# Layer 3's per-batch mixing on half-height, half-width products, with one bias product per block

## The chip, the cores and the metric

One core of a Trainium2 chip. The metric is the time of one execution in microseconds (us) on the device. All data are float32. The core has TensorE (PE, whose weight loads are listed apart as PEld), VectorE (DVE), ScalarE (ACT), GpSimd (POOL) and SyncE (SP), which here only issues DMAs.

## The reference, cut to what matters

Four layers follow each other on an activation x of 32 batches, 64 channels and 1024 features. Each adds to x a function of x and of a conditioning vector of 128 numbers per batch. Layers 0 and 3 first mix the channels of each batch with a matrix of its own:

```python
att = jax.nn.softmax((h @ W2 + b2) / T, axis=-1)        # 32 batches x 8
agg_w = jnp.einsum('bk,koi->boi', att, weight[..., 0])  # a 64x64 matrix per batch
agg_b = att @ bias_k                                    # 64 biases per batch
out = jnp.einsum('boi,bih->boh', agg_w, x) + agg_b[:, :, None]
```

In layer 3, whose mixing is changed, what comes out goes into a feed-forward part: an up product from 1024 to 2048 and 512 features, a down product back to 1024, a gate that sums the two largest of 8 logits, and a layer norm. Layers 1 and 2 mix by a grouped convolution. Layer 2's feed-forward part sends each row (a channel of a batch) to two of 16 experts, and gathers the two results per row at the end.

## The kernel before, in words

The 2048 rows (32 batches x 64 channels) lie in 16 tiles of 128 rows, so that a tile holds two batches: batch 2j in partitions 0 to 63 and batch 2j+1 in partitions 64 to 127. The work of a tile is named by j, its 8 chunks of 128 features by c.

Layer 3 goes in 4 blocks b of 4 tiles (t = 0 to 3). `blended` (L541) makes the mixed activation of a block, transposed: for a tile it multiplies a bias product (L547: `ones` of 8 rows by `bbs[t]`, which `mixed_bias` (L214) has made on GpSimd out of the attention weights and `bk3`), copies that to SBUF on ScalarE (L549), and then takes, for each chunk, the 128x128 piece of x as the stationary operand and `aw[:, t, :]` as the streamed one (L554). `aw` for a tile is 128x128 with the two batches' 64x64 matrices on its diagonal and zeros elsewhere, which `mixing` (L195) has laid out during layer 2 and stored in DRAM (`awd`). Four chunks go to one bank of PSUM; VectorE adds the bias and writes the sum into one of four quarters of y (L555). `quarters` (L515, its adds at L517 to L520) then makes four sums and differences of quarters, which the seven-product scheme of `seven` (L899) needs in the up (L954, products at L964) and down products (L1000, products at L1019).

Block 0 is mixed at the end of layer 2's part. There `gather` (L528) loads a tile of x3 and fetches the two expert results per row by indirect DMAs on GpSimd's queue (`fetch`, L525; L526), `merge` (L535) adds the three on VectorE (L537) and stores the sum as x4 (L538); its tiles come from `slot_b`, the pool `pb` of 8 buffers (L76), which also holds `aw0` (L817) and the layer-2 features yT of the last tiles until `base2` (L665, products at L670, adds at L676, store of x3 at L678) has used them. At most two gathers are asked for ahead (L820, L828). Once block 0 is mixed the pools of the early layers are closed, and layer 3's tiles lie where they were: gw (L840), aw (L854) and the up weights (`prepared`, L933) are loaded on SyncE's queue behind the stores of layer 2.

Blocks 1 to 3 are mixed by `mixed` (L851) in the middle of the block before: `down(b, 1, ...)` calls `meanwhile` after its second product "2" (L1027), and that calls `mixed(b + 1)` and `gate(b + 1)` (L858, products at L864). `mixed` loads the x4 tiles with `loaded` into a tag `xm` of two buffers, so that the load of the third tile waits until the first has been multiplied. The gate's copy `gs` (L867) has one buffer; `best` (L871) reads it at the start of the next block.

The order in which each engine's instructions stand in its queue isn't written out by hand: the framework sets it when the program is built, by the order of the source and by what it estimates to be ready, and it assigns buffers of a pool as it goes. An engine then works through its queue in that order and waits on semaphores.

The other names that the prediction uses: L611 is layer 2's routing product (80 streamed columns), L744 a transpose, L754 the expert products (64 rows at a time, the two halves of the array by turns), L915 to L921 the sums of `seven` (u_u, v_u, v_d), L842 and L844 loads of gamma and beta.

Of the kernel before, what the change touches and what calls it, by code (L numbers as in the profile page):

```python
# [28 lines left out]
F32 = mybir.dt.float32  # L29
# [4 lines left out]
ALU = mybir.AluOpType  # L34
AX = mybir.AxisListType

P = 128
D = 1024
NT = 16
NC = D // P  # L40
HF = 512
TB = 512
# [4 lines left out]
KC = 8  # L47
# [11 lines left out]
QUARTER = {(0, 0): 0, (1, 0): 1, (1, 1): 2, (0, 1): 3}  # L59
# [5 lines left out]
def four_layers(ctx: ExitStack, tc: tile.TileContext, a: dict, out: bass.AP):  # L65
    nc = tc.nc

    cst = ctx.enter_context(tc.tile_pool(name="cst", bufs=1))
    small = ctx.enter_context(tc.tile_pool(name="small", bufs=2))
# [9 lines left out]
    def slot_a(name):  # L79
        return pa.tile([P, D], F32, tag="a", name=name)  # L80

    def slot_b(name):
        return pb.tile([P, D], F32, tag="b", name=name)

    def bank(name, shape=(P, HF), dtype=F32):
        return psp.tile(list(shape), dtype, tag="ps", name=name)

    def const(name, src, shape, eng=None):
        t = cst.tile(list(shape), F32, name=name)
        (eng or nc.gpsimd).dma_start(out=t, in_=src)  # L90
        return t
# [6 lines left out]
    ones = cst.tile([P, P], F32, name="ones")  # L98
# [25 lines left out]
    att = {}  # L124
    with tc.tile_pool(name="mlp", bufs=1) as mp:
        mlp = {}
        for n in (0, 3):
            mlp[n] = {}
            for k, shape in (("W0", (P, P)), ("b0", (P, 1)), ("W1", (P, P)), ("b1", (P, 1)), ("W2", (P, KC))):
                t = mp.tile(list(shape), F32, name=f"{k}_{n}")  # L130
                nc.sync.dma_start(out=t, in_=a[f"{k}_{n}"])
                mlp[n][k] = t
            t = mp.tile([NB, KC], F32, name=f"b2_{n}")
# [4 lines left out]
        for n in (0, 3):  # L138
            m = mlp[n]
            ps = bank(f"mlp0_{n}", (P, NB))  # L140
# [3 lines left out]
            ps = bank(f"mlp1_{n}", (P, NB))  # L144
# [3 lines left out]
        for n in (0, 3):  # L148
            ps = bank(f"mlp2_{n}", (NB, KC))
# [15 lines left out]
            ps = bank(f"attT_{n}", (P, NB))  # L165
# [48 lines left out]
    def mixed_bias(n, j, bk, eng):  # L214

        bb = small.tile([KC, 2, 64], F32, tag="row", bufs=8, name=f"bb_{n}_{j}")
        eng.tensor_tensor(
            bb,
            att[n][:KC, ts(j, 2), None].to_broadcast([KC, 2, 64]),
            bk[:, None, :].to_broadcast([KC, 2, 64]),  # L220
            ALU.mult,
        )
        return bb.rearrange("k b o -> k (b o)")
# [28 lines left out]
    with tc.tile_pool(name="q", bufs=1) as qp, tc.tile_pool(name="w", bufs=NC) as wq:  # L252
# [6 lines left out]
        with tc.tile_pool(name="l0", bufs=1) as lp, tc.tile_pool(name="s0", bufs=2) as sp:  # L259
# [7 lines left out]
            zs, lhs, whs, whTs, rows, bbs, cbs = {}, {}, {}, {}, {}, {}, {}  # L267
# [102 lines left out]
            aw = lp.tile([P, NT, P], F32, name="aw_0")  # L370
# [9 lines left out]
            ps = bank("rsum", (KC, E0 + P))  # L380
# [132 lines left out]
    bk3 = const("bk_3", a["bk_3"], (KC, 64))  # L513

    def quarters(t, r):  # L515
        tt = nc.vector.tensor_tensor
        tt(t[0], r[3], r[0], ALU.subtract)  # L517
        tt(t[1], r[2], t[0], ALU.subtract)
        tt(t[2], r[2], r[3], ALU.subtract)
        tt(t[3], r[1], t[1], ALU.subtract)  # L520
# [7 lines left out]
    def gather(j, tile3):  # L528
        got = [tile3(f"m{i}_{j}") for i in range(3)]
        nc.sync.dma_start(out=got[0], in_=x3[j])  # L530
        for k in range(2):
            fetch(got[1 + k], outs[:, :], slot[:, k, j : j + 1])
        return got

    def merge(j, got):  # L535
# [2 lines left out]
        nc.sync.dma_start(out=x4[j], in_=got[0])  # L538
        return got[0]

    def blended(b, aw, tiles, bbs):  # L541

        y = [slot_a(f"y3_{b}_{q}").rearrange("p (c t) -> p c t", t=HT) for q in range(8)]
        for t in range(4):
            j = 4 * b + t
            ps = bank(f"ab_{j}", (P, P))
            nc.tensor.matmul(ps, ones[:KC, :], bbs[t], start=True, stop=True)  # L547
            ab = small.tile([P, P], F32, tag="row", bufs=8, name=f"abs_{j}")
            nc.scalar.copy(ab, ps)  # L549
            xt = tiles(t)  # L550
            for h in range(2):
                ps = bank(f"mix_{j}_{h}", (P, 4, P))
                for c in range(4):
                    nc.tensor.matmul(ps[:, c, :], xt[:, ts(4 * h + c, P)], aw[:, t, :], start=True, stop=True)  # L554
                nc.vector.tensor_tensor(  # L555
                    y[QUARTER[h, t // 2]][:, :, ts(t % 2, P)], ps, ab[:, None, :].to_broadcast([P, 4, P]), ALU.add
                )
        quarters(y[4:8], y[0:4])
        return y

# [3 lines left out]
    with (  # L564
# [212 lines left out]
        for j in range(NT + 1):  # L777
# [13 lines left out]
            if j == 4:  # L791
                aw = [wp.tile([P, NT // 2, P], F32, tag="bg", bufs=3, name=f"aw3_{i}") for i in range(2)]
# [23 lines left out]
                base2(*late.pop(0))  # L816
        aw0 = slot_b("aw3_now")[:, : 4 * P].rearrange("p (t o) -> p t o", o=P)  # L817
        nc.sync.dma_start(out=aw0, in_=awd[:, 0:4, :])
        bbs = [mixed_bias(3, j, bk3, nc.gpsimd) for j in range(4)]
        got = [gather(j, slot_b) for j in range(2)]  # L820
        for j in range(AMID - 2, AMID):
            for n in range(2):
# [2 lines left out]
        def now(j):  # L825
# [3 lines left out]
            return t  # L829

        y = blended(0, aw0, now, bbs)

    early.close()
    l3 = ctx.enter_context(ExitStack())
    lp = l3.enter_context(tc.tile_pool(name="l3", bufs=1, reuse_waits="tile"))
# [10 lines left out]
    def loaded(j, name, bufs):  # L846
        t = wp.tile([P, D], F32, tag=name, bufs=bufs, name=f"{name}_{j}")
        nc.sync.dma_start(out=t, in_=x4[j])
        return t

    def mixed(b):  # L851

        aw = lp.tile([P, 4, P], F32, tag="aw", name=f"aw_{b}")
        nc.sync.dma_start(out=aw, in_=awd[:, ts(b, 4), :])  # L854
        bbs = [mixed_bias(3, j, bk3, nc.gpsimd) for j in range(4 * b, 4 * b + 4)]
        return blended(b, aw, lambda t: loaded(4 * b + t, "xm", 2), bbs)

    def gate(b, y):  # L858

        gp = bank(f"gp_{b}", (P, 2, HT))  # L860
        for half in range(2):
            for c in range(NC):
                q = ds(32 * (c % 4), 32)
                nc.tensor.matmul(  # L864
                    gp[q, half, :], gw[:, c, :], y[QUARTER[c // 4, half]][:, c % 4, :], start=(c < 4), stop=(c >= 4)
                )
        gs = lp.tile([P, TB], F32, tag="gs", name=f"gs_{b}")  # L867
        nc.scalar.copy(gs, gp.rearrange("p h t -> p (h t)"))
        return gs
# [216 lines left out]
    gs = gate(0, y)  # L1086
    for b in range(NBL):
        tot = [wp.tile([P, D], F32, tag="tot", bufs=4, name=f"tot_{b}_{t}") for t in range(4)]
        hs = [up(b, 0, y, None)]
        dgs = best(b, gs)  # L1090
        hs.append(up(b, 1, y, None))
        sg = spread_best(b, dgs)
        hs += [up(b, g, y, None) for g in range(2, HG)]
        down(b, 0, hs, tot, lambda: None)
        hs = []
        got = None
        for g in range(HG, NG):
            if b + 1 < NBL:
                j = 4 * b + 4 + g - HG
                if got:  # L1100
                    merge(j - 1, got)
                got = gather(j, merged) if g < HG + 4 else None
            hs.append(up(b, g, y, sg))
        ahead = []

        def meanwhile():
            if b + 1 < NBL:
                ahead.append(mixed(b + 1))
                ahead.append(gate(b + 1, ahead[0]))

        xs = residual(b)
        down(b, 1, hs, tot, meanwhile)
        if ahead:
            y, gs = ahead
        finish(b, tot, xs)
# [87 lines left out]
```

## Time and profile before

| | us |
|---|---|
| median of 3 runs | 1860.04 (1858.42 to 1861.30) |
| the profiled execution | 1869.54 |
| its span (first to last instruction) | 1867.8 |
| TensorE busy in it | 1740.9 (93%) |
| VectorE busy | 807.9 (43%) |
| mixing products of layer 3, blocks 1 to 3 (L554, 192 instructions) | 24.4 |
| the same, block 0 (64 instructions) | 11.1 |
| bias products (L547, 32 instructions) | 8.0 |
| bias adds (L555, 32 instructions) | 21.6 |

Times in the views are microseconds from the start of the span, unless ns is said. A row of a timeline gives start, length, engine, line of the kernel, operation, the tile written and those read, the size, and how many instructions the row merges; in square brackets stands how long the engine was idle before it and what ended that. A row of the chain gives start, length and what the time went to; "issue" is time for which the profile shows no cause. TensorE's lengths are from entry to the modelled end, so that a row's length holds a tail that overlaps the next row: what an instruction costs is read from start to start. A float32 product is two instructions on TensorE, each with a weight load.

### The profile page before, as it was taken

How to read it: one execution, taken by the hardware profiler on the slowest of the kernel's cores; microseconds unless marked ns; L12 is line 12 of the kernel's file. 1: busy time of each engine (PE TensorE's matmuls, PEld its weight loads, DVE VectorE, ACT ScalarE, POOL GpSimd, SP SyncE). 2: the span in 40 equal slices, each digit the busy share in tenths (PEclk: the TensorE clock that was granted, in tenths of full speed). 3: DMA queues.
4: the chain of work that ended last, by engine and by line, in shares of the span. 5: the costliest groups of instructions: out<-in, count | busy, mean ns of one | idle time of the engine just before them, and what ended most of it. 6: DMA issues, size and time to landing. Idle time of an engine off the chain costs nothing.

```text
span 1867.8 us, 20908 instructions
## 1 busy us (share of the span) xinstructions
PE 1740.9 (93%) x7526; PEld 1166.0 (62%) x7526; DVE 807.9 (43%) x1700; ACT 203.0 (11%) x547; POOL 600.6 (32%) x628
## 2 busy tenths in 40 slices
PE   7997779989999999898879999999999999999996
PEld 6576657766776433585357567486585685684862
DVE  1577799836655333463243361022541123620223
ACT  1100044200000122010000100000010000000000
POOL 2245535542432553244223142023141132320230
PEclk9999889989999999999989999999999999999998
DMA  8894321056662599888876574445564444644432
GB/s 297 265 280 85 58 68 46 1 147 192 188 177 87 184 355 353 292 297 299 280 254 215 160 241 148 150 150 162 176 209 158 148 154 140 232 152 152 147 96 96
DMA packets 185910, 340.48 MB, mean 182 GB/s; under 512 B 20432, under 2 KB 91872, under 8 KB 185808
## 3 DMA queue, kind: packets, MB, share of 16 engines
q1 hardware_dynamic: 171712, 295.76, 50.3%
q0 software_dynamic: 14096, 43.39, 7.1%
q8 instruction: 60, 0.98, 0.2%
q14 instruction: 42, 0.34, 0.1%
HBM read 238.28 MB, written 83.89 MB: 172 GB/s over the span
## 4 chain that ended last, share of the span: by engine, by line
PE 71%; DMA 11%; issue 7%; DVE 5%; POOL 3%; SPq 2%; ACT 0%; POOLq 0%; DVEq 0%; ACTq 0%
PE p_d L1019 23%; PE p_u L964 22%; PE o L670 8%; PE conv L239 5%; DMA m<-x 4%; PE oo L480 3%; PE lr L611 2%; PE fold L358 1%; DMA x<-m 1%; PE ex L754 1%; DMA g<-x 1%; DMA m<-outs,slot 1%; POOL x L489 1%; POOL lo L473 1%; PE mix L554 1%
## 5 line engine op out<-in xcount | busy, mean ns | idle before, releaser
L1019 PE MATMUL p_d<-dn,h 128*128 128x512 f32 x1120 | 487.4, 596 | 7.2 <-DVE v_d L921 3.8
L1019 PEld LDWEIGHTS p_d<-dn,h 128*128 128x128 f32 x1120 | 213.1, 191 | 274.3 <-issue 267.8
L964 PE MATMUL p_u<-y,up 128*128 128x256 f32 x1680 | 366.7, 380 | 6.0 <-DVE v_u L921 6.0
L964 PEld LDWEIGHTS p_u<-y,up 128*128 128x128 f32 x1680 | 319.3, 191 | 53.0 <-DVE v_u L921 7.2
L670 PE MATMUL o<-base,yT 128*128 128x512 f32 x512 | 225.5, 595 | 0.6 <-DVE eo L757 0.4
L670 PEld LDWEIGHTS o<-base,yT 128*128 128x128 f32 x512 | 95.4, 191 | 118.5 <-issue 115.0
L239 PE MATMUL conv<-cw,g 128*128 128x128 f32 x1024 | 129.3, 288 | 4.7 <-DMA g<-x 3.2
L239 PEld LDWEIGHTS conv<-cw,g 128*128 128x128 f32 x1024 | 126.7, 205 | 5.3 <-DMA g<-x 3.4
L480 PE MATMUL oo<-cbt,lo 128*128 128x512 f32 x256 | 103.6, 405 | 4.1 <-POOL lo L473 3.9
L480 PE MATMUL oo<-cbt,hi 128*128 128x512 f32 x256 | 104.5, 408 | 0.0
L977 POOL TENSOR_TENSOR raw<-u_u,v_u 128x256 f32<-128x256 f32 x40 | 31.5, 788 | 211.1 <-DVE v_u L921 211.0
L964 PE MATMUL p_u<-y,r 128*128 128x256 f32 x240 | 62.9, 414 | 24.3 <-DVE v_u L921 22.2
L537 DVE TENSOR_TENSOR m<-m,m 128x1024 f32<-128x1024 f32 x32 | 39.3, 1228 | 101.9 <-DMA m<-x 84.2
L676 DVE TENSOR_TENSOR xo<-x,o 128x256 f32<-128x256 f32 x64 | 35.4, 594 | 105.1 <-PE o L670 93.0
L526 POOL DMA_INDIRECT m<-outs,slot x32 | 38.4, 1200 | 125.8 <-DVE m L537 90.1
L921 DVE TENSOR_TENSOR v_u<-e_u,p_u 128x256 f32<-128x256 f32 x40 | 16.8, 419 | 136.2 <-PE p_u L964 136.2
L992 POOL TENSOR_TENSOR h<-h 128x256 f32<-128x256 f32 x40 | 29.5, 738 | 137.4 <-DVE h L986 100.8
L964 PE MATMUL p_u<-y,s 128*128 128x256 f32 x320 | 72.2, 379 | 0.0
L964 PEld LDWEIGHTS p_u<-y,r 128*128 128x128 f32 x240 | 49.3, 209 | 35.6 <-DVE v_u L921 24.6
L330 POOL TENSOR_TENSOR x<-x,bias 128x512 f32<-128x512 f32 x32 | 37.1, 1177 | 102.7 <-DMA g<-x 99.6
L921 DVE TENSOR_TENSOR v_d<-e_d,p_d 128x512 f32<-128x512 f32 x16 | 10.9, 687 | 127.4 <-PE p_d L1019 127.4
L964 PEld LDWEIGHTS p_u<-y,s 128*128 128x128 f32 x320 | 60.8, 190 | 8.3
(243 smaller groups left out, 2092.7 us busy)
## 6 DMA issues: line engine op xcount, KB each, us to landing
dn<-ds SPq DMA_DIRECT2D x160, 256.0 KB
up<-us SPq DMA_DIRECT2D x60, 512.0 KB
outs<-eo SPq DMA_DIRECT2D x48, 512.0 KB
dn<-in_dn_dram SPq DMA_DIRECT2D x96, 256.0 KB
g<-x SPq DMA_DIRECT2D x256, 64.5 KB
up<-in_up_dram SPq DMA_DIRECT2D x30, 512.0 KB
ds<-sum SPq DMA_DIRECT2D x20, 512.0 KB
us<-s SPq DMA_DIRECT2D x20, 512.0 KB
```

The costliest lines, as they stand in the source:

```text
L239: nc.tensor.matmul(ps[:, g, :], rows[:, 4 * b + g, ds(w, P)], cwt[:, g, w, :], start=(w == 0), stop=(w == 1))
L330: nc.gpsimd.tensor_tensor(xh(j, h), xh(j, h), halved(bias1[:, ts(h, HF)]), ALU.add)
L480: nc.tensor.matmul(po, terms[j][i][:, c, :], cbt[c][:, ts(n, HF)], start=(c == 0 and i == 0), stop=(c == NC - 1 and i == 1),)
L526: nc.gpsimd.indirect_dma_start(out=dst, out_offset=None, in_=src, in_offset=rows_of(at))
L537: nc.vector.tensor_tensor(got[0], got[0], got[1 + k], ALU.add)
L611: nc.tensor.matmul(ps, yT[j][:, c, :], ra2[:, c, :], start=(c == 0), stop=(c == NC - 1))
L670: nc.tensor.matmul(po, yT[j][:, c, :], base[c][:, ts(n, HF)], start=(c == 0), stop=(c == NC - 1))
L676: nc.vector.tensor_tensor(new, old[:, ts(n, 64), :], add, ALU.add)
L964: nc.tensor.matmul(ps[0], ws[i][:, k, c, :], y[RHS[p]][:, c, :], start=(start and c == 0), stop=(c == 3), skip_group_check=not start,)
L977: nc.gpsimd.tensor_tensor(raw[:, 1, 1], m["u"], m["v"], ALU.add)
L992: tt(h[:, 4], h[:, 1], h[:, 3], ALU.add)
L1019: nc.tensor.matmul(ps[q], hs[k][:, HLHS[p], ts(q, P)], ws[k], start=(start and k == 0), stop=(k == HG - 1), skip_group_check=not start,)
```

## The change

In `blended`, the bias of a block is one product: `block_bias` makes all 8 batches' weighted biases in one GpSimd operation, in a tile of 8 rows and 512 columns, one TensorE product of 512 columns follows, and four ScalarE copies. Each chunk of a tile is multiplied as two products of 64 rows and 64 streamed columns: partitions 0 to 63 by the first batch's matrix, partitions 64 to 127 by the second's, into two banks of PSUM, one per batch, each with all 8 chunks. The zeros of `aw` are no longer multiplied. VectorE's add takes one batch and four chunks at a time, so there are four of 128x256 per tile where there were two of 128x512. The new bias tile is a buffer of `slot_b` in block 0, and of the tag `gs` in the others.

```diff
+    def block_bias(b, t):
+        bb = t[:KC, : 4 * P].rearrange("k (t o) -> k t o", o=P)
+        nc.gpsimd.tensor_tensor(
+            bb.rearrange("k t (h o) -> k (t h) o", h=2),
+            att[3][:KC, ts(b, 8), None].to_broadcast([KC, 8, 64]),
+            bk3[:, None, :].to_broadcast([KC, 8, 64]),
+            ALU.mult,
+        )
+        return bb
+
     def blended(b, aw, tiles, bbs):
 
         y = [slot_a(f"y3_{b}_{q}").rearrange("p (c t) -> p c t", t=HT) for q in range(8)]
+        pa_ = bank(f"ab_{b}", (P, 4, P))
+        nc.tensor.matmul(pa_, ones[:KC, :], bbs.rearrange("k t o -> k (t o)"), start=True, stop=True)
+        abq = [small.tile([P, P], F32, tag="row", bufs=8, name=f"abs_{b}_{t}") for t in range(4)]
+        for t in range(4):
+            nc.scalar.copy(abq[t], pa_[:, t, :])
         for t in range(4):
             j = 4 * b + t
-            ps = bank(f"ab_{j}", (P, P))
-            nc.tensor.matmul(ps, ones[:KC, :], bbs[t], start=True, stop=True)
-            ab = small.tile([P, P], F32, tag="row", bufs=8, name=f"abs_{j}")
-            nc.scalar.copy(ab, ps)
+            ab = abq[t]
             xt = tiles(t)
+            ps = [bank(f"mix_{j}_{g}", (P, NC, 64)) for g in range(2)]
+            for c in range(NC):
+                for g in range(2):
+                    q = ds(64 * g, 64)
+                    nc.tensor.matmul(ps[g][:, c, :], xt[q, ts(c, P)], aw[q, t, q], start=True, stop=True)
             for h in range(2):
-                ps = bank(f"mix_{j}_{h}", (P, 4, P))
-                for c in range(4):
-                    nc.tensor.matmul(ps[:, c, :], xt[:, ts(4 * h + c, P)], aw[:, t, :], start=True, stop=True)
-                nc.vector.tensor_tensor(
-                    y[QUARTER[h, t // 2]][:, :, ts(t % 2, P)], ps, ab[:, None, :].to_broadcast([P, 4, P]), ALU.add
-                )
+                for g in range(2):
+                    q = ds(64 * g, 64)
+                    nc.vector.tensor_tensor(
+                        y[QUARTER[h, t // 2]][:, :, ds(t % 2 * P + 64 * g, 64)],
+                        ps[g][:, ts(h, 4), :],
+                        ab[:, None, q].to_broadcast([P, 4, 64]),
+                        ALU.add,
+                    )
         quarters(y[4:8], y[0:4])
         return y
...
-        bbs = [mixed_bias(3, j, bk3, nc.gpsimd) for j in range(4)]
+        bbs = block_bias(0, slot_b("bb3_0"))
...
-        bbs = [mixed_bias(3, j, bk3, nc.gpsimd) for j in range(4 * b, 4 * b + 4)]
-        return blended(b, aw, lambda t: loaded(4 * b + t, "xm", 2), bbs)
+        return blended(b, aw, lambda t: loaded(4 * b + t, "xm", 2), block_bias(b, lp.tile([P, TB], F32, tag="gs", name=f"bb3_{b}")))
```

## The prediction

> **What bounds the kernel now.** I read the page's totals and its chain first, then the timeline of TensorE around the mixing of blocks 1 to 3, then rows that show what a half-array product costs, then the handover from layer 2 to layer 3, where block 0 is mixed.
>
> ```profile
> PE 1740.9 (93%) x7526; PEld 1166.0 (62%) x7526; DVE 807.9 (43%) x1700; ACT 203.0 (11%) x547; POOL 600.6 (32%) x628
> ...
> PE 71%; DMA 11%; issue 7%; DVE 5%; POOL 3%; SPq 2%; ACT 0%; POOLq 0%; DVEq 0%; ACTq 0%
> ```
>
> TensorE is busy for 93% and is 71% of the chain, so what it is spared inside layer 3 is worth its full time, unless another wait comes up there. Now the timeline of TensorE in block 1 (start, length, ..., number of instructions):
>
> ```profile
> 1044.90 0.48 PE L547 MATMUL ab<-bb,ones 8*128 8x128 f32 x2
> 1045.31 2.05 PE L554 MATMUL mix<-aw,xm 128*128 128x128 f32 x16
> 1047.29 0.48 PE L547 MATMUL ab<-bb,ones 8*128 8x128 f32 x2
> 1047.71 2.05 PE L554 MATMUL mix<-aw,xm 128*128 128x128 f32 x16
> 1049.69 0.48 PE L547 MATMUL ab<-bb,ones 8*128 8x128 f32 x2
> 1050.75 2.02 PE L554 MATMUL mix<-aw,xm 128*128 128x128 f32 x16 [0.57 <-DMA xm<-x]
> 1052.70 0.48 PE L547 MATMUL ab<-bb,ones 8*128 8x128 f32 x2
> 1053.15 2.02 PE L554 MATMUL mix<-aw,xm 128*128 128x128 f32 x16
> 1055.11 1.50 PE L864 MATMUL gp<-y,gw 128*32 128x256 f32 x24
> ```
>
> Each product shows as two instructions (8 chunks, x16), each with a weight load of its own. A tile's bias product takes 0.41 us until the next row starts, a tile's mixing 1.98. From the first bias product to the gate (L864) it is 10.21 us; blocks 2 and 3 have 10.33 and 10.46. The third tile waits 0.57 us for xm: there are two buffers, its load is issued at 1047.39 when the first tile is done with one, and lands in time for 1050.75, 3.36 us later. That wait is what counts below.
>
> **Part 1: the mixing on TensorE.** 16 instructions of 128 rows and 128 streamed columns per tile become 32 of 64 rows and 64 columns. Two things must be known: what paces such instructions, and whether the two halves run side by side.
>
> ```profile
> 504.25 1.91 PE L611 MATMUL lr<-ra,yT 128*128 128x80 f32 x16
> 505.99 0.33 PE L642 MATMUL rk<-both,before 128*128 128x16 f32 x2
> ...
> 632.21 1.99 PE L754 MATMUL ex<-bg,bTs 64*128 64x512 f32 x8 [0.29 <-ACT bTs L746]
> 634.13 0.33 PE L744 MATMUL bT<-ident,bin 128*128 128x128 f32 x1
> ```
>
> L611 streams only 80 columns, and its 16 still take 1.74 us, 0.109 each, against 0.112 for the mixing with 128 (the loads of a tile take 1.86 us for 16, one 0.19: 1.67/15 = 0.111). So the pace is that of the weight load of 128 columns, and fewer streamed columns gain nothing. L754 multiplies 64 rows at a time on alternate halves, as the change will: 8 instructions of 512 columns end within 1.92 us, 0.24 each, where full-height ones of 512 columns take 0.43 (L670: 64 from 746.27 to 773.94). So halves run side by side, and their four first loads take 0.30 us together where one takes 0.18: two at a time. I take 32 instructions in pairs at 0.112 a pair, 1.79 us a tile, what the 16 take today: **no gain from the halves**. The lower bound is that the streams alone pace it (64/128 of 0.107 a pair, 0.86 a tile), against which L611 speaks; the upper that loads do not pair when the stream is short, 32 x 0.112 = 3.57 a tile.
>
> [...]
>
> **Part 2: one bias product per block.** Four of 0.41 go (1.64 us); one of 512 columns comes: 0.41 + 2 x (0.43 - 0.11) = 1.05 us. The tiles then follow each other without a change between, which spares about 0.1 us of entry and 0.1 of exit at each; these are in the 1.98.
>
> **Sum for blocks 1 to 3**, from the first bias instruction: bias to 1.05; tile 0 to 2.94 (0.1 entry + 1.79); its buffer's load is issued at 3.04 and lands for 6.40; tile 1 to 4.73; tile 2 6.40 to 8.29, with 1.67 us of waiting; tile 3's load, issued at 4.83, is there at 8.19; tile 3 to 10.08; gate at 10.18 against 10.21. The product saved is **eaten by the xm load**, for the first tile now frees its buffer 0.55 us later, behind the longer bias product. Blocks 2 and 3, whose fourth tile also waits for its load, gain some 0.1 each. All three: -0.2 us. Lower bound, if the streams pace it: tile 0 ends at 2.0, the load lands at 5.5, tiles 2 and 3 run to 7.5: -2.7 a block, -8 in all.
>
> VectorE: 8 adds of 128x512 (0.598 from start to start when queued) become 16 of 128x256 (L921, one of that size out of PSUM, lasts 0.419; less the 0.094 by which L555's 0.692 exceeds its pitch: 0.325), +0.4 us a block. It has idle time beside the mixing (9.64 of 13.3 us busy). Both halves of a tile now share banks, and the adds may have to wait for the whole tile: then the last four end at about 10.1 + 4 x 0.325 = 11.4, ahead of the last gate products, which today start at 12.70 after two instructions of the down product. Nothing. Were that cover gone, up to 1.3 us a block. GpSimd (four of 0.39 to one of four times the length) and ScalarE (four copies of 0.266 in a row while tile 0 is mixed) are idle there. The bias's new tile shares the one buffer of gs, long read by then, and is read before the next gate copy.
>
> **Part 3: block 0.** There the bias takes one of the 8 buffers of pool b (line 76). Two views, GpSimd's and then the chain:
>
> ```profile
> 758.23 0.95 POOL L526 DMA_INDIRECT m<-outs,slot  x1 [0.30 <-issue]
> 761.46 0.94 POOL L526 DMA_INDIRECT m<-outs,slot  x1 [2.29 <-DVE m L537]
> 765.07 0.94 POOL L526 DMA_INDIRECT m<-outs,slot  x1 [2.66 <-DVE m L537]
> ```
>
> ```profile
> 784.85 0.32 SPq L678
> ...
> 787.86 6.80 DMA r<-in_up_dram
> 794.66 0.14 issue
> 794.80 1.98 PE p_u L964 x8
> ```
>
> Held at that time: yT of tiles 12 and 13 (base2, until 774) and aw0. That leaves five: two m0 and three fetches. The trace agrees: fetches 1 to 3 go back to back (755.67, 756.98, 758.23), the fourth waits for the first merge add (759.97 + 1.23). With one buffer less, the third does: 761.46 instead of 758.23. It landed after 4.17 us (762.40), so now at 765.63; its add goes from 763.57 to 765.65, and the fifth fetch, which waited for that add, slips by 2.1 with it. By way of its adds and the seventh fetch (773.12) hang the add at 780.47, base2's adds queued behind it on VectorE, the store of x3 (784.85, L678), and behind it on SyncE gw, aw and the first up weights, for which TensorE waits 1.70 us until 794.80. After that it is busy (33.5 of 34 us). I take **+2.1**. Bounds: +4.1, if the sixth fetch must wait for the fourth's add as well; -1.7, if base2's adds come to stand ahead of the stalled merge add, so that the weights land early and the gate's end (793.1) decides. The shorter bias (0.7 us before tile 3) and the 12 queued adds (+0.4) lie beside the weights' 6.80 us.
>
> Forecast: -0.2 + 2.1 = +1.9 on the profiled execution, 1869.54 us (span 1867.8). That one lies 9.5 above the median of the runs, 1860.04, so I carry the difference over: 1862.
>
> **Rivals.**
> (B) *Loads do not pair*: 3.57 us a tile; gate at 1.05 + 0.1 + 14.3 + 0.1 = 15.5, so +5.3, +5.2, +5.0, and 2 to 3 in block 0 (two tiles fit ahead of 782.8): +18, **1878**, slower. The point from which it decides is 2.0 us a tile. For it: no row shows 64-row loads with so short a stream. Against: L754's loads in pairs. It is also the case that the halves do not do what the change says.
> (C, D) *VectorE's queue in block 0's up products shifts.* From 820 to 990 the merge adds of later blocks wait for their loads (84.2 us, 12 times) with v_u queued behind them, and TensorE waits for v_u 22.2 us, 6 times, longest 10.8. Their places are set when the program is built, from costs that this change alters. One wait more is 3.7 us by the mean: **1866**, slower (C); one or two fewer, or the bound of Part 1: 1862 - 7.4, **1854**, faster (D).
>
> **Chances.** Forecast 0.50 (own range 1857 to 1867; of it 0.37 within 0.2%, 0.11 above, 0.02 below), B 0.16, C 0.14, D 0.20 (0.17 faster, 0.03 same). Faster than 1856.3: 0.19; within 0.2%, about what a measurement can tell: 0.40; slower than 1863.8: 0.41. The range 1854 to 1879 reaches from D's middle to B and leaves out some 0.15.
>
> **What would show it.** Mixing rows at some 1.8 us a tile (3.6: B; under 1.2: D); a third tile that waits 1.2 us or more for xm; gate within 0.3 us of 10.2 after the first bias row; the third fetch of block 0 waiting for a merge add and the first p_u some 2 us later against the end of the expert stage; TensorE's waits for v_u near 22 us. If those move by over 4 us, the forecast is wrong for a reason that the change's own operations do not hold.

## The result, and the profile after

The change makes the kernel slower: a median of 1885.79 us over 5 runs (1880.82 to 1889.59) against 1860.04 (1858.42 to 1864.11), a ratio of 1.0133 with a 95% interval of 1.0113 to 1.0154. The forecast was 1862, and the time lies above the range that was given (1854 to 1879). The profiled execution of after took 1889.59 us (span 1887.8), 20 more than that of before, and the stages below are compared between these two. By the medians the change costs 25.7 us: the profile of before lay 9.5 above its median, that of after 3.8, so the account below is of 20 of them.

The page's totals after, for those of before:

```profile
PE 1749.4 (93%) x7758; PEld 1171.5 (62%) x7758; DVE 811.3 (43%) x1732; ACT 201.6 (11%) x547; POOL 602.8 (32%) x616
...
PE 45%; DMA 8%; DVE 4%; issue 1%; SPq 0%; ACT 0%; DVEq 0%; POOLq 0%
```

TensorE is as busy as before, which hides the loss: its instructions have become longer in some stretches. The shares of the chain add up to only 58% here, so I go by stages instead. From the start of the last expert product to the first up product of block 0 it was 49.0 us and is 58.5: +9.5. The stretch from the first bias product of a block's mixing to the last gate product was 13.0, 13.1 and 13.2 us in blocks 1 to 3 and is 17.3, 18.0 and 16.5: +12.6. What lies ahead of that last expert product moved by +1.7, all the rest by -3.8, and the sum is 20.

TensorE's timeline in block 1 after, for the one shown of before:

```profile
1055.01 1.12 PE L555 MATMUL ab<-bb,ones 8*128 8x512 f32 x2
1056.06 3.79 PE L567 MATMUL mix<-aw,xm 64*128 64x64 f32 x64
1061.39 7.09 PE L567 MATMUL mix<-aw,xm 64*128 64x64 f32 x64 [1.54 <-DVE y L571]
1068.41 2.68 PE L882 MATMUL gp<-y,gw 128*32 128x256 f32 x24
1071.03 1.12 PE L1037 MATMUL p_d<-dn,h 128*128 128x512 f32 x2
```

The first 64 instructions, two tiles, take 3.79 us, a tail included: 1.8 us a tile, as forecast. Then TensorE waits, as forecast too: the third tile starts 6.38 us after the bias product (forecast 6.40). The bracket puts the end of that wait to VectorE's adds, the releaser that was last by the profile. But in all three blocks of after the third tile starts 0.135 us after the last semaphore update of its load (1061.255 in block 1), and so it does in before, so it is the load that ends the wait. What the forecast had no term for comes then: the same 64 instructions take 7.09 us, and the gate's 24 take 2.68 where they took 1.50. They run at half the clock: the record of the granted clock has 0.50 from 1060.62 to 1070.86. In block 2 the clock falls ahead of the wait, at 1320.0, within the first two tiles:

```profile
1317.38 4.70 PE L567 MATMUL mix<-aw,xm 64*128 64x64 f32 x64
1322.67 7.09 PE L567 MATMUL mix<-aw,xm 64*128 64x64 f32 x64 [0.59 <-DVE y L571]
```

A table of the three blocks' stretches shows the clock (start and end, length, busy time of TensorE, its loads, VectorE, ScalarE, GpSimd, then the granted clock, the DMA share and GB/s):

```profile
1055.00:1072.70 17.70, 16.16 (x166) 12.37 (x165) 10.32 (x22) 0.77 (x4) 0.00 (x0) 0.71 0.49 163
1316.30:1334.90 18.60, 18.01 (x166) 13.64 (x166) 11.26 (x23) 0.88 (x5) 0.00 (x0) 0.63 0.48 158
1578.30:1595.40 17.10, 15.05 (x166) 11.35 (x166) 10.35 (x22) 0.87 (x5) 2.36 (x1) 0.80 0.37 126
```

The column to read is the one after GpSimd's: 0.71, 0.63 and 0.80, in blocks where before has 1.00 throughout:

```profile
1044.90:1058.20 13.30, 12.72 (x108) 9.78 (x107) 9.64 (x14) 1.06 (x4) 0.00 (x0) 1.00 0.60 184
```

GpSimd's timeline in block 0 after:

```profile
757.37 0.95 POOL L526 DMA_INDIRECT m<-outs,slot  x1 [22.27 <-issue]
758.62 0.95 POOL L526 DMA_INDIRECT m<-outs,slot  x1 [0.30 <-issue]
763.27 0.95 POOL L526 DMA_INDIRECT m<-outs,slot  x1 [3.70 <-DVE m L537]
765.76 0.94 POOL L526 DMA_INDIRECT m<-outs,slot  x1 [1.55 <-DVE m L537]
768.96 0.94 POOL L526 DMA_INDIRECT m<-outs,slot  x1 [2.25 <-DVE m L537]
775.11 0.94 POOL L526 DMA_INDIRECT m<-outs,slot  x1 [5.21 <-DVE m L537]
782.51 0.94 POOL L526 DMA_INDIRECT m<-outs,slot  x1 [6.45 <-DVE m L537]
788.80 0.94 POOL L526 DMA_INDIRECT m<-outs,slot  x1 [5.35 <-DVE m L537]
```

Every fetch from the third on waits for a merge add, and the last three go one at a time: fetch, landing, add, next fetch. The eighth goes at 788.80 where it went at 775.32. Until its add is done TensorE stands idle for 9.5 us. Later the load of gw lands at 802.28, and the gate's 32 products then run at half the clock (0.50 from 784.14 to 808.03): 3.64 us where they took 1.97, so that up to 1.7 of the 9.5 us that block 0 loses are the clock's.

### The profile page after: what moved, and what is told of

Same layout as the page of the kernel before. It is cut to its first block, busy times and chain, and to the rows that moved or that the text cites. A ratio compares the mean times of both kernels' runs of the same rounds, so it can differ in the third digit from the quotient of the medians.

```text
span 1887.8 us, 21396 instructions
## 1 busy us (share of the span) xinstructions
PE 1749.4 (93%) x7758; PEld 1171.5 (62%) x7758; DVE 811.3 (43%) x1732; ACT 201.6 (11%) x547; POOL 602.8 (32%) x616
## 4 chain that ended last, share of the span: by engine, by line
PE 45%; DMA 8%; DVE 4%; issue 1%; SPq 0%; ACT 0%; DVEq 0%; POOLq 0%
PE p_d L1037 22%; PE p_u L982 20%; DMA m<-x 4%; DMA x<-m 2%; PE mix L567 2%; DVE m L537 1%; DMA m<-outs,slot 1%; DVE tot L1095 1%; PE gp L882 1%; DMA r<-in_up_dram 1%; DVE st L1089 0%; DMA dn<-gd 0%; DMA gw<-in_gw_dram 0%; DVE tot L1072 0%; DMA xm<-x 0%
## 5 line engine op out<-in xcount | busy, mean ns | idle before, releaser
L480 PE MATMUL oo<-cbt,lo 128*128 128x512 f32 x256 | 104.3, 407 | 4.0 <-POOL lo L473 3.8
L480 PE MATMUL oo<-cbt,hi 128*128 128x512 f32 x256 | 105.1, 411 | 0.0
L982 PE MATMUL p_u<-y,r 128*128 128x256 f32 x240 | 62.4, 412 | 22.6 <-DVE v_u L939 22.2
```

Of the source, the lines that this page charges most:

```text
L480: nc.tensor.matmul(po, terms[j][i][:, c, :], cbt[c][:, ts(n, HF)], start=(c == 0 and i == 0), stop=(c == NC - 1 and i == 1),)
L982: nc.tensor.matmul(ps[0], ws[i][:, k, c, :], y[RHS[p]][:, c, :], start=(start and c == 0), stop=(c == 3), skip_group_check=not start,)
```

## The experiments

Two theories came out of this, each with a rival. For block 0: the bias's tile takes a buffer that the fetches need (rival: the half products, their shared banks and 16 adds delay it). For blocks 1 to 3: the clock is halved because TensorE stands idle at the third tile (I), or because short streams under full-width loads keep the array too little busy (D). The second pair fell in that form; a third theory (A) is told after the first four runs. "Bias to gate" below is from a block's first bias row to its first gate row, "handover" from the last expert product to the first up product. Before has 10.21, 10.34 and 10.46, and 49.0. The first four kernels have one set of 13 runs of before beside them (median 1861.00), the last four another of 23 (1862.44).

**bias_only**: the new bias product, the mixing of before.

```diff
+        pa_ = bank(f"ab_{b}", (P, 4, P))
+        nc.tensor.matmul(pa_, ones[:KC, :], bbs.rearrange("k t o -> k (t o)"), start=True, stop=True)
...
-            ps = bank(f"ab_{j}", (P, P))
-            nc.tensor.matmul(ps, ones[:KC, :], bbs[t], start=True, stop=True)
...
-        bbs = [mixed_bias(3, j, bk3, nc.gpsimd) for j in range(4)]
+        bbs = block_bias(0, slot_b("bb3_0"))
```

(against before; the copies and the other blocks as in the change)

> The bias part alone: one bias product per block, with its tile in a buffer of pool b in block 0; the mixing is full height as before. Theory (the buffer taken from pool b makes block 0's fetches go one after another): from the third fetch on each waits for a merge add, the first up product comes 8 to 11 us later after the end of the expert stage than before, and the whole is 1866 to 1871. Rival (block 0 is late because of the half products, their shared banks and 16 adds): block 0 within 2 us of before, 1857 to 1861. In blocks 1 to 3 both expect the granted clock to stay at 1.00 and the gate within 0.5 us of 10.2 after the first bias row.

Measured 1879.48 us, ratio 1.0090 (1.0066 to 1.0114); handover 57.7 us, 8.6 more than before. Its time lies above both expectations. In its profile 3.4 us more than in that of before went to block 0's up products, where TensorE waited 25.8 us for v_u instead of 22.2 (what rival C described, here and not in after), and 0.9 to each of the others' mixing; that is a part of the excess, and the rest isn't located. Block 1 of it, TensorE:

```profile
1059.32 1.12 PE L555 MATMUL ab<-bb,ones 8*128 8x512 f32 x2
1060.37 3.84 PE L566 MATMUL mix<-aw,xm 128*128 128x128 f32 x32
1065.72 2.02 PE L566 MATMUL mix<-aw,xm 128*128 128x128 f32 x16 [1.52 <-DMA xm<-x]
1068.48 2.02 PE L566 MATMUL mix<-aw,xm 128*128 128x128 f32 x16 [0.74 <-DVE y L567]
1070.44 1.50 PE L875 MATMUL gp<-y,gw 128*32 128x256 f32 x24
```

TensorE idles as long as in after (1.52 us) and once more, and yet a tile takes 2.02 us after the wait and the gate 1.50: the clock stayed at 1.00 in all three blocks. So **idle time of this length alone didn't halve it**. Bias to gate is 11.1 to 11.3, not 10.2: the fourth tile's load landed 0.9 us later than I reckoned (its last semaphore update is at 1068.35, 0.135 us ahead of the tile, though the bracket names an add).

**halves_only**: the half products and their adds, the bias of before.

```diff
-                    nc.tensor.matmul(ps[:, c, :], xt[:, ts(4 * h + c, P)], aw[:, t, :], start=True, stop=True)
...
+                    nc.tensor.matmul(ps[g][:, c, :], xt[q, ts(c, P)], aw[q, t, q], start=True, stop=True)
```

> The half-height products alone, with a bias product per tile as before and no buffer taken from pool b. Block 0 by the buffer theory within 2 us of before; by its rival 8 to 11 us late. In blocks 1 to 3 the third tile waits for its load about as long as before (0.6 us). Theory I (the clock is halved because TensorE stands idle for some 1.7 us at the third tile): the clock stays at 1.00 there and the blocks cost what they did, 1858 to 1862 in all. Theory D (the clock is halved because short streams of 64 columns under loads of 128 keep the array too little busy): 0.50 in the middle of the mixing also here, 3 to 5 us a block, 1869 to 1875.

Measured 1876.90 us, ratio 1.0080 (1.0063 to 1.0097); handover 50.8 us, 1.7 more than before, which the buffer theory asks for. Block 1:

```profile
1047.13 0.48 PE L547 MATMUL ab<-bb,ones 8*128 8x128 f32 x2
1048.14 2.00 PE L555 MATMUL mix<-aw,xm 64*128 64x64 f32 x32 [0.52 <-DMA xm<-x]
1050.07 0.48 PE L547 MATMUL ab<-bb,ones 8*128 8x128 f32 x2
1050.56 3.76 PE L555 MATMUL mix<-aw,xm 64*128 64x64 f32 x32
1054.24 2.79 PE L871 MATMUL gp<-y,gw 128*32 128x256 f32 x24
```

A wait of 0.52 us, no longer than before's 0.57, and the fourth tile takes 3.76 us: halved here too, in all three blocks (mean clock from the first bias product to the last gate product 0.79, 0.79 and 0.60), for 3.1, 2.8 and 7.5 us more than before up to the last gate product. Theory I falls. D's sum (3 to 5 a block) is nearly met in blocks 1 and 2 and exceeded in block 3, and the time lies above D's range (1869 to 1875).

**after_g8**: the whole change with another place for block 0's bias.

```diff
-        bbs = block_bias(0, slot_b("bb3_0"))
+        bbs = block_bias(0, gp8.tile([P, NS, SEG], F32, tag="g8", name="bb3_0").rearrange("p s i -> p (s i)"))
```

> The whole change, but block 0's bias tile lies in a buffer that layer 2 no longer needs (the tag g8), so that pool b keeps its 8 buffers for the fetches. Buffer theory: the third fetch goes back to back with the second again, the first up product is within 2 us of before after the expert stage, blocks 1 to 3 still lose some 4 us each: 1871 to 1876. Rival (half products are what delays block 0): no gain, 1882 to 1888.

Measured 1872.49 us, ratio 1.0071 (1.0046 to 1.0096); handover 48.5 us, 10.0 less than after. GpSimd's first fetches:

```profile
748.59 0.95 POOL L526 DMA_INDIRECT m<-outs,slot  x1 [21.45 <-issue]
749.85 0.94 POOL L526 DMA_INDIRECT m<-outs,slot  x1 [0.30 <-issue]
751.10 0.94 POOL L526 DMA_INDIRECT m<-outs,slot  x1 [0.30 <-issue]
754.62 0.94 POOL L526 DMA_INDIRECT m<-outs,slot  x1 [2.58 <-DVE m L537]
757.88 0.94 POOL L526 DMA_INDIRECT m<-outs,slot  x1 [2.32 <-DVE m L537]
759.13 0.95 POOL L526 DMA_INDIRECT m<-outs,slot  x1 [0.30 <-issue]
```

Three fetches back to back again, and from there on all eight within 0.25 us of before's, seen from the end of the expert stage. **The buffer is block 0's whole loss**; its rival falls. The clock is halved in blocks 1 to 3 as in after (bias to gate 12.9 to 13.6, and in block 1 the fourth tile takes 3.76 us).

**after_g8_raw**: that, and no tile waits for its load.

```diff
-        return blended(b, aw, lambda t: loaded(4 * b + t, "xm", 2), ...)
+        return blended(b, aw, lambda t: loaded(4 * b + t, "xm" if t < 2 else "raw", 2), ...)
```

> As after_g8, and the third and fourth tile of blocks 1 to 3 are loaded into two buffers of the tag raw, which are free at that time, so that no tile waits for its load. Theory I (idle time halves the clock): the clock stays at 1.00, a block's gate comes some 8.3 us after its first bias row (1.05 + 4 x 1.79 + 0.1) against 10.2 before, and the whole is 1852 to 1857. Theory D (short streams halve the clock): it is halved all the same within the 7 us of mixing, the gate comes 10 to 13 us after the first bias row, 1864 to 1873.

Measured 1860.23 us over 10 runs that lie widely (1851.29 to 1869.23), ratio 1.0006 (0.9985 to 1.0026). In its profile, that of the shortest run, the clock is 1.00 and bias to gate 8.34 us in all three blocks, as theory I asked, but the median isn't what I asked by that theory. Block 1:

```profile
1035.13 1.12 PE L555 MATMUL ab<-bb,ones 8*128 8x512 f32 x2
1036.18 3.79 PE L567 MATMUL mix<-aw,xm 64*128 64x64 f32 x64
1039.80 3.74 PE L567 MATMUL mix<-aw,raw 64*128 64x64 f32 x64
1043.47 1.62 PE L882 MATMUL gp<-y,gw 128*32 128x256 f32 x24
```

So neither idle time alone (1.52 us in bias_only) nor, in this profile, short streams alone halved the clock; the change has both. The trace records when the granted clock changes: of the 15 stretches at 0.50 in before's, 4 last 3.41 us, 7 last 6.83, 2 last 10.24 and one 17.07, the last reaches the end, and all changes lie on one grid of 3.413 us, to 2 ns, as they do in after's. So I counted by windows of that grid, and worked out for each the share of it in which the array streams, each product counted by its rows over 128. The length of a wait alone doesn't sort the cases: waits of 1.54 us (after) and 0.52 us (halves_only) were followed by the half clock, one of 1.52 us (bias_only) wasn't. An instruction of 512 columns takes 0.43 us here (L670 of before), so by my estimate 128 columns stream in some 107 ns and 64 in 53. Full-height mixing then streams 107 of its 112 ns, half-height 53 of 112: 0.48, before any wait. That gave theory A: a window with a share under some 0.4 is followed by half the clock, whatever the products' shape. It was put to a test without any half product:

**before_xm1**: before with one buffer for xm.

```diff
-        return blended(b, aw, lambda t: loaded(4 * b + t, "xm", 2), bbs)
+        return blended(b, aw, lambda t: loaded(4 * b + t, "xm", 1), bbs)
...
-            xr = loaded(j, "xm", 2) if j == NT - 1 else loaded(j, "xr", 3)
+            xr = loaded(j, "xm", 1) if j == NT - 1 else loaded(j, "xr", 3)
```

> The kernel before with one buffer instead of two for the tiles that blocks 1 to 3 mix: each tile's load waits for the tile before, full-height products as before. Theory A (the clock is granted by how much of each 3.4 us the array streams, counted by rows; it is halved below some 0.4, whatever the shape of the products): a tile of 1.8 us in every 5.4 or so is a share of some 0.33, so 0.50 appears within the mixing of every block, tiles then take 3.5 us, and the gate comes 20 to 26 us after the first bias row. Rival H (only half-height products together with idle time halve it): 1.00 throughout, gate 17 to 20 us after the first bias row.

One run, 1900.84 us. Block 1:

```profile
1040.58 2.05 PE L554 MATMUL mix<-aw,xm 128*128 128x128 f32 x16
1042.56 0.48 PE L547 MATMUL ab<-bb,ones 8*128 8x128 f32 x2
1045.84 2.02 PE L554 MATMUL mix<-aw,xm 128*128 128x128 f32 x16 [2.79 <-DMA xm<-x]
1047.79 0.48 PE L547 MATMUL ab<-bb,ones 8*128 8x128 f32 x2
1051.10 3.65 PE L554 MATMUL mix<-aw,xm 128*128 128x128 f32 x16 [2.82 <-DMA xm<-x]
1054.67 0.48 PE L547 MATMUL ab<-bb,ones 8*128 8x128 f32 x2
1058.07 3.64 PE L554 MATMUL mix<-aw,xm 128*128 128x128 f32 x16 [2.91 <-DMA xm<-x]
```

Full-height products go at half clock in every block (mean clock 0.86, 0.81 and 0.63 from the first bias product to the last gate product), in block 1 from the third tile on and in blocks 2 and 3 from the second (3.61 and 3.75 us); bias to gate is 21.5 to 23.5 us. Theory A holds and H falls. Over the mixing of all kernels up to here and the next one, windows at full clock with shares of 0.00 to 0.38 were followed by the half clock, save one of 0.37; none was from 0.39 up. The bound is blurred by about 0.02, as my sums are. It isn't peculiar to the mixing. Counted in the same way over all ten whole profiles of this case, from 33 us on, where the clock records begin (L480's products at their own pace of 0.23 us), every window at full clock with a share up to 0.35 was followed by the half clock and none from 0.39 up; between these, 6 were and 4 were not.

**after_g8_raw_again**: the same kernel, a second profile, for its spread.

> The same kernel as after_g8_raw, for a second profile: its times lay between 1851 and 1869, more widely than those of before, and the first profile was of the shortest. If the spread comes from layer 3's blocks 1 to 3, the gate is no longer at 8.34 or the clock no longer at 1.00 there; if it comes from earlier stages or from block 0's up products, those three blocks repeat to 0.1 us and another stretch has moved.

One run, 1858.08 us. Blocks 1 and 2 repeat to the hundredth (8.34). Block 3 does not:

```profile
1545.77 1.12 PE L555 MATMUL ab<-bb,ones 8*128 8x512 f32 x2
1546.82 4.96 PE L567 MATMUL mix<-aw,xm 64*128 64x64 f32 x64
1551.57 7.04 PE L567 MATMUL mix<-aw,raw 64*128 64x64 f32 x64
1558.54 2.79 PE L882 MATMUL gp<-y,gw 128*32 128x256 f32 x24
```

No wait, and still half the clock from 1549 on, for 6.4 us more up to the last gate product (17.6 against 11.2). The window before it, from 1545.8, held the bias product, whose 8 rows of 128 hardly count, and half-height mixing: a share of 0.34. In the first profile the corresponding window began half a microsecond ahead of the bias product, on the end of the down product, came to 0.39, and nothing happened. So **the half products sat at the bound** in these two profiles, and where the windows fell decided. Block 2 of after was such a case too: the clock fell there ahead of the wait, behind a window of 0.38. Three blocks with 0 or 6.4 us each would give a spread like the one measured; that it comes from there alone isn't shown.

**bias_g8_raw**: full-height mixing, one bias product outside pool b, no waits: bias_only with the edits of after_g8 and after_g8_raw.

```diff
-        bbs = block_bias(0, slot_b("bb3_0"))
+        bbs = block_bias(0, gp8.tile([P, NS, SEG], F32, tag="g8", name="bb3_0").rearrange("p s i -> p (s i)"))
...
-        return blended(b, aw, lambda t: loaded(4 * b + t, "xm", 2), ...)
+        return blended(b, aw, lambda t: loaded(4 * b + t, "xm" if t < 2 else "raw", 2), ...)
```

> Full-height mixing, one bias product per block with block 0's bias tile outside pool b, and the third and fourth tile of blocks 1 to 3 loaded into free buffers of another tag, so that no tile waits. All theories: gate at 1.05 + 4 x 1.8 + 0.1 = 8.3 to 8.5 us after the first bias row, clock at 1.00; block 0 within 2 us of before. 1.8 to 2.1 us less per block: 1853 to 1858. If the half products gain anything by themselves, the same kernel with them has its gate earlier than this one's.

Measured 1857.13 us (1849.27 to 1864.38, 12 runs), ratio 0.9975 (0.9957 to 0.9992): the one version here that beats before, by a quarter of a per cent. Block 1:

```profile
1047.69 1.12 PE L555 MATMUL ab<-bb,ones 8*128 8x512 f32 x2
1048.74 3.84 PE L566 MATMUL mix<-aw,xm 128*128 128x128 f32 x32
1052.41 3.74 PE L566 MATMUL mix<-aw,raw 128*128 128x128 f32 x32
1056.08 1.50 PE L875 MATMUL gp<-y,gw 128*32 128x256 f32 x24
```

Bias to gate is 8.39 in all blocks at clock 1.00. With half products it was 8.34 at that clock: they gain 0.05 us a block up to there, and up to the last gate product they are 0.07 behind (11.21 against 11.14). They bring nothing in exchange for the risk. Handover 49.6 us.

**before_raw**: before with only the free buffers.

```diff
-        return blended(b, aw, lambda t: loaded(4 * b + t, "xm", 2), bbs)
+        return blended(b, aw, lambda t: loaded(4 * b + t, "xm" if t < 2 else "raw", 2), bbs)
```

> The kernel before with nothing but the free buffers for the third and fourth tile of blocks 1 to 3. The waits of 0.6 to 0.8 us per block go and the four bias products stay: gate at 4 x 2.39 + 0.1 = 9.6 to 9.7 us after the first bias row, 1857 to 1860 in all. The rest to the version with one bias product (1.3 us a block) is then the bias product's share.

Measured 1861.12 us, ratio 0.9997 (0.9985 to 1.0010), above the 1857 to 1860 expected. Bias to gate 9.58 as expected, but the 2.3 us that the three blocks gain by that isn't told from no change by its time. One bias product is the other 1.2 us a block (8.39).

## Why the prediction was wrong

**Right.** The halves run side by side with short streams too, a pair of instructions in 0.112 us, as long as one full-height instruction takes: 1.8 us a tile, no gain (8.34 against 8.39 above). Rival B falls. The blocks' sum held up to the third tile (6.38 us for 6.40, its load issued at 3.12 for 3.04), and the saved bias product was eaten by the xm load. The extra adds on VectorE cost nothing that shows (same 8.34). In block 0 the third and the fifth fetch slipped as worked out: 3.23 and 2.1 us by the forecast, 3.31 and 2.16 against the end of the expert stage (the fourth, for which it has no figure, 2.57).

**Wrong, the larger part: "Sum for blocks 1 to 3 ... -0.2 us"; measured +12.6.** Of that, 8.6 lie ahead of the gate and 4.0 in the gate's own products and what stands between them. The step took every duration at the clock that before's trace shows in these blocks, and checked the new wait only for its length. In the count by windows that wait (1.67 us forecast) and streams of half the length are the same quantity: time in which the array streams nothing. I had both numbers, 53 of 112 ns a pair and 1.67 us idle, and did not put them together: 2.6 us of mixing in a window of 3.41 at 0.48 is a share of 0.37 (0.34 in the trace of block 1). In block 2 not even the wait was needed: the bias product of 8 rows and half-height mixing filled a window to 0.38. The trace of before showed that clock falling elsewhere, 15 times; its rows at 0.5 were not looked at for what had preceded them. That trace held the bound: from 33 us on, the 15 windows at full clock that the half clock followed in it had shares of 0.33 or less, all others 0.40 or more.

**Wrong, the smaller part: "I take +2.1" in block 0; measured +9.5** (10.0 by after_g8), beyond the step's bound of 4.1. The first fetch that was late was right, and so was its cause. What failed was carrying its slip through unchanged. With a buffer less, the fetches no longer go in pairs: the sixth waits for the fourth's add (which I had as the bound), the fourth's data took 7.85 us from issue to its add instead of 5.38, the seventh then waits for the sixth's add where it waited for the fifth's, the eighth for the seventh's. Seen from the end of the expert stage they are 7.1, 7.7 and 11.7 us late. So a buffer less in this ring cost not once but again as the ring came round: 3.3 us at the third fetch, 11.7 at the eighth. Up to 1.7 of the 9.5 us are the gate's products at half the clock, for which the step had no term either.

**Rivals C and D** did not come: TensorE waited for v_u 22.2 us in block 0's up products before and after.

## What to carry to other kernels

Before splitting a product into half-height or short-stream pieces, or adding a wait beside one, work out what share of each 3.4 us the array will stream, weighted by rows: in this case's traces every window at full clock with a share up to 0.35 was followed by 3.41 us or more at half of it and none from 0.39 up, and the pieces themselves were at 0.48. With loads of 128 columns, instructions of 80 and of 128 streamed columns took 0.11 us each here, and so did a pair of 64: fewer streamed columns saved nothing. A buffer borrowed from a pool that a chain of fetches goes round in can be paid for more than once: look at each later fetch for the add that it will then wait for.

## What the runs showed of the hardware that was not expected

The granted clock fell to half without any idle time, in block 3 of after_g8_raw_again and in block 2 of after, and after a wait of 0.52 us in halves_only, while 1.52 us of idle time amid full-height products left it at full in bias_only. Once it had fallen, it came back in the mixing only once full-height products, the gate's among them, had run (in the three blocks of after 2.45, 4.00 and 1.91 us behind the gate's first): half-height mixing kept it there, and in block 3 of halves_only the stretch at half lasted 17.1 us, gate included. Coming back took a larger share than staying at full in these traces. Counted as above, but by the columns of the array in use as well (the gate uses 32 of 128), windows at half clock with a share up to 0.73 were all followed by another in the ten profiles, and all from 0.78 up by the full clock; half-height mixing at half clock has a share of 0.50 at most.
